# Keeping the transposed w1 of two expert layers in DRAM between two feedforwards, and clearing k's grouped rows in parts

## The chip, the cores and the metric

The kernel runs on one core of one Trainium2 chip. The metric is the device time of one execution in microseconds (us), as the median of several runs. A core has five engines that run their own instruction streams: TensorE (PE in the profile; PEld is its weight load), VectorE (DVE), ScalarE (ACT), GpSimd (POOL) and SyncE (SP), which here only issues DMAs. ScalarE and GpSimd issue DMAs too. All transfers share 16 DMA engines.

## The reference

The input x is 4 x 1024 tokens of 256 values, in float32. The result is

```
x = x + 0.5 * ffn(layernorm(x))
x = x + attn(layernorm(x))
x = x + 0.5 * ffn(layernorm(x))      # the same weights again
```

`ffn` normalizes its input once more to xn and makes q, k and v with three "fast feedforward" layers, then takes softmax(q k^T / 16) v + xn as y, and returns y plus a fourth such layer (f) of y. One fast feedforward is a routed layer: each token walks down a binary tree of depth 8 (255 node vectors), and ends at one of 256 leaves, each with its own little network:

```
for _ in range(DEPTH):
    logit = jnp.einsum('bsd,bsd->bs', x, nw[node]) + nb[node]
    node = 2 * node + 1 + (logit > 0).astype(jnp.int32)
leaf = node - NN
h = act(jnp.einsum('bsd,bsdl->bsl', x, w1[leaf]) + b1[leaf])      # w1: 256 x 256 x 16
return jnp.einsum('bsl,bsld->bsd', h, w2[leaf]) + b2[leaf]        # w2: 256 x 16 x 256
```

The weights of q, k, v and f are the same in both feedforwards. `attn` is a multi-head attention with rotary positions and a page-wise causal mask; the change does not touch it.

## The kernel before, in words

`ffn` (L822) is called twice, with `first=True` (L1687) and `first=False` (L1689), with `attention` between them.

**Routing.** `routes` (L382) goes over the 4096 tokens in eight steps of four tiles of 128 tokens. A step transposes the tokens (L331), multiplies them with all node vectors at once (L340), compares, and finds the leaf by two more matrix products (L354, L366). `routes` overlaps four steps and calls a function `before(k)` once per step, in which other work is woven in.

**Placing and scattering.** `place` (L493) counts the tokens per block of eight leaves and gives each token a row, so that each block's rows fill whole tiles of 128. `scattering` (L580) writes the tokens to these rows of a DRAM buffer `xs` with indirect DMAs from GpSimd (L573), a tile each. `xs` has 63 tiles of rows; rows with no token must be zero, so in the first feedforward `clear` (L268) writes zeros over them first. q and v share one `xs` buffer, k has its own (`xs[1]`).

**w1.** The first weights of the leaves are needed with the 256 inputs on the partitions. `load_first` (L625) makes this out of four parts of 1 MB each (`raw`, two buffers): a part is transposed in four groups of four 128x128 transpositions on TensorE (L636), each group copied out of PSUM by ScalarE (L641) or VectorE (L639) into the SBUF tile `w1` (one buffer, 4 MB). When a part is used up, the next is loaded (L643, L601). The third part waits until the first has been transposed. The 16 groups are woven into a routing, three per step from step 1 on: q's into k's routing (`beside`, L932), k's into v's routing (`building`, L963). v's is made in one go after k's leaves.

**Leaves.** `leaves` (L668) goes over the grouped tiles. For each it loads the rows (`xg`, L677, four tiles ahead), transposes them (L683), multiplies with the block's w1 (L701) and b1 (L704), masks (L709), transposes (L719), applies the activation (L721), multiplies with w2 (L726), and stores the result to DRAM (`og`, L739). Beside the leaves of q run the placing and the scatters of k; beside those of k the placing and scatters of v. `with_steps` (L854) takes one step of the side work per leaf tile.

**What sets the order.** Outside the last attention of `ffn` a scheduler orders each engine's instructions by its own reckoning, within the dependences; `keep_in_program_order` pins single instructions. SyncE issues its DMAs one after another, in the order that this gives: in the first feedforward x, the clear of q's `xs`, two parts of q's w1, the clear of k's `xs`, then the load of q's tile count into a register (L652), a clear of the spare rows of k's results, two more parts, w2 of q (L591), a clear of the spare rows of q's results, two parts of k's w1, and the first xg. [...]

Of the kernel before, what the change touches and what calls it, by code (L numbers as in the profile page):

```python
# [15 lines left out]
F32 = mybir.dt.float32  # L16
# [55 lines left out]
def macaron_kernel(ctx: ExitStack, tc: tile.TileContext, a: dict, out: bass.AP):  # L72
# [183 lines left out]

    xs += [xs[0], dram.tile([NSLOT, XW + 1], F32, name="xs_f")]
    ytok = dram.tile([NTOK, E], F32, name="ytok")


    SPARE = (48, 53, 58, NGRP)
# [6 lines left out]
    def clear(queue, rows):  # L268
        n, width = rows.shape
        return queue.dma_start(  # L270
            rows.rearrange("(g p) c -> p g c", p=P), bc(zero[:, :width], 1, n // P)
        )
# [220 lines left out]
    def place(pool, oh, acc, rows, gblk, sel):  # L493


        ng = tiles_of(pool, counts(pool, acc, NT))
        yield
        end = ends_of(pool, "gend", ng, 0.0)
        first = first_row(pool, end, ng)
        yield  # L500
        for h in range(2):
            yield from ranks(pool, oh, acc, rows, h * NT // 2, (h + 1) * NT // 2, first)
            yield
        found = []
        yield from blocks_ended(pool, acc, NT, found)
        yield
        tile_blocks(pool, found[0], end, gblk, sel)
# [72 lines left out]
    def scattering(f, slot, rows, n):  # L580

        views = dram_disjoint_views(xs[f], NT)
        for t in range(0, NT, n):
            scatter(f, slot, rows, views, *range(t, min(t + n, NT)))
            yield
# [18 lines left out]
    def load_raw(pool, f):  # L604

        return [load_part(pool, f, *p) for p in PART[:2]]
# [18 lines left out]
    def load_first(pool, f, w1, raws, on_both=True):  # L625

        nb_half = P // EPB
        for k, (hf, c) in enumerate(PART):
# [4 lines left out]
            for l0 in range(0, LW, 4):  # L633
# [9 lines left out]
                    raws.append(load_part(pool, f, *PART[k + 1 + len(raws)]))  # L643
                yield

    PRE = 4
    REGS = 16

# [173 lines left out]
    def ffn(first: bool, last: bool):  # L822
# [3 lines left out]
        def drain(*gens):  # L826
            for g in gens:
                for _ in g:
                    pass
# [6 lines left out]
        with ExitStack() as es:  # L836
# [17 lines left out]
            def with_steps(main, *sides):  # L854
# [3 lines left out]
                    next(side, None)  # L858
                drain(side)

            qs = ExitStack()
            with ExitStack() as ws, banks(0, 8):
                wp, lp = stage(ws, "w", 1), stage(ws, "leaves", 2)
# [7 lines left out]
                with ExitStack() as hs, ExitStack() as rs:  # L871
                    raw = stage(rs, "raw", 1, "right")
                    pp = stage(hs, "place", 1)
                    with ExitStack() as rt:
                        hp = stage(rt, "head", 2)
                        scale = [None] * NT
                        if first:
                            mom = hp.tile([P, NT, 2], F32, name="mom", bufs=1)
                        else:
                            mom = moments[1]  # L880

                        def norms(k):
                            ts_ = range(k * GT, k * GT + GT)
                            if first:
                                t = k * GT
                                nc.sync.dma_start(
                                    xres[:, t : t + GT, :],
                                    a["x"][
                                        t // TPB, (t % TPB) * P : (t % TPB + GT) * P, :
                                    ].rearrange("(i p) e -> p i e", p=P),  # L890
                                )
                                for t in ts_:
                                    rows_moments(hp, mom[:, t, :], xres[:, t, :])
                                sc = both_norms(hp, mom[:, k * GT : k * GT + GT, 1], GT)
                            else:

                                lo = k * GT
                                if lo in (0, NT - TPB):
                                    n = TPB if lo else NT - TPB
                                    sc = both_norms(hp, mom[:, lo : lo + n, 1], n, f"_{n}")  # L900
                                    scale[lo : lo + n] = [sc[:, i : i + 1] for i in range(n)]
                                sc = None
                            for i, t in enumerate(ts_):
                                nc.vector.tensor_scalar(
                                    x_of(t),
                                    xres[:, t, :],
                                    mom[:, t, 0:1],
                                    scale[t] if sc is None else sc[:, i : i + 1],
                                    ALU.subtract,
                                    ALU.mult,  # L910
                                )

                        hot = hots_of(pp, 0, 2)
                        routes(hp, 0, *hot, leaf[0], norms)
                        if first:
                            clear(nc.sync, xs[0])
                        w1 = w1_of(0)
                        ahead = load_raw(raw, 0)
                        if first:
                            tc.keep_in_program_order(clear(nc.sync, xs[1]))  # L920
                        build = load_first(raw, 0, w1, ahead)
                        rows = []
                        drain(place(pp, *hot, rows, gblk[0], sel[0]))
                        going = scattering(0, slot[0], rows, 5)
                        hot = hots_of(pp, 1, 2)

                        if first:
                            b1s = [load_b1(raw, f) for f in range(len(FFFS))]
                            for g in b1s[:2]:
                                next(g)  # L930

                        def beside(k):  # L932
                            drain(islice(build, 3 * (k > 0)), islice(going, 1))
                            if first and k and k % 2 == 0:
                                f = k // 2 - 1
                                drain(b1s[f])
                                if f + 2 < len(FFFS):
                                    next(b1s[f + 2])

                        routes(hp, 1, *hot, leaf[1], beside)  # L940
                        drain(build, going)
                        if first:
                            drain(*b1s)
                        w2 = load_second(nc.sync, wp, 0)
                        if first:
                            tc.keep_in_program_order(clear(nc.sync, osrt[0][SPARE[0] * P :]))
                        what = tree(0, AF.Relu, w1, w2)
                        ahead = load_raw(raw, 1)
                        rows = []
                        with_steps(  # L950
                            leaves(*what),
                            place(pp, *hot, rows, gblk[1], sel[1]),
                            scattering(1, slot[1], rows, 1),
                        )
                        spare_leaves(*what)
                        if first:
                            tc.keep_in_program_order(clear(nc.sync, osrt[1][SPARE[0] * P :]))
                        w1 = w1_of(1)
                        build = load_first(raw, 1, w1, ahead)
                        hot = hots_of(pp, 2, 2)  # L960
                        w2 = None

                        def building(k):  # L963
                            nonlocal w2
                            drain(islice(build, 3 * (k > 0)))
                            if k == 4:
                                w2 = load_second(nc.scalar, wp, 1)

                        routes(hp, 2, *hot, leaf[2], building)
                        drain(build)  # L970

                    raw2 = stage(hs, "raw2", 1)
                    what = tree(1, AF.Relu, w1, w2)
                    ahead = load_raw(raw, 2)
                    ahead += [load_part(raw2, 2, *p) for p in PART[2:]]
                    rows = []
                    with_steps(
                        leaves(*what),
                        place(pp, *hot, rows, gblk[2], sel[2]),
                        scattering(2, slot[2], rows, 1),  # L980
                    )
                    spare_leaves(*what)
                    if first:
                        tc.keep_in_program_order(clear(nc.sync, osrt[2][SPARE[0] * P :]))
                    w1 = w1_of(2)
                    w2 = load_second(nc.scalar, wp, 2)
                    drain(load_first(raw, 2, w1, ahead))
                    tc.no_sync_barrier()
# [741 lines left out]
```

## Time and profile before

| what | value |
|---|---|
| median of three runs | 2568.53 us (2558.93 to 2577.99) |
| the profiled execution | 2818.15 us; its span, from first to last instruction, 2816.4 us |
| TensorE (PE) busy | 2399.0 us, 85% |
| VectorE / ScalarE / GpSimd busy | 1472.2 / 1062.7 / 856.4 us |
| moved by DMA | 321.02 MB, mean 114 GB/s |
| clear of `xs` of q and k | 2 DMAs of 8095.5 KB |
| parts of w1 of q, of k | 8 DMAs of 1024.0 KB each (both feedforwards) |

The profile is of one execution, which is longer than the runs without a profile. Busy times are summed per engine; an instruction that issues a DMA counts as not busy, and its duration is that of the issuing. The timeline gives for each instruction its start, its duration, its engine and line, what is written from what, and in brackets how long the engine was idle before it and who released it. An engine that is not the bottleneck loses nothing by being idle, so a share of busy time says little: the stretch in question has to be looked at.

### The profile page before, as it was taken

The page shows a single profiled execution, that of the slowest core. Times are in us where ns is not written, and L with a number is a line of the kernel's source. Part 1 is how long each engine was busy: PE and PEld are TensorE (multiplying, and loading weights), DVE is VectorE, ACT ScalarE, POOL GpSimd, SP SyncE. Part 2 cuts the span into 40 slices and gives each one's busy share as a digit, 9 for nine tenths or more (in the row PEclk, how much of TensorE's full clock was granted, in tenths as well). Part 3 has the DMA queues.
Part 4 walks back from the last instruction along what each step waited for, and adds up shares of the span by engine and source line. Part 5 has one row for each costly group of instructions (what it writes and reads, how often), then busy time and mean ns, then how long its engine had stood idle before and what let it go on. Part 6 is the DMA issues. An engine that isn't in the chain of part 4 may idle for free. (4 is left out here: it accounts for less than half of the span.)

```text
span 2816.4 us, 43155 instructions
## 1 busy us (share of the span) xinstructions
PE 2399.0 (85%) x14456; PEld 1507.2 (54%) x14456; DVE 1472.2 (52%) x4382; ACT 1062.7 (38%) x2495; POOL 856.4 (30%) x978
## 2 busy tenths in 40 slices
PE   7789887877897879999999999889898887879884
PEld 3466776545565744434343443346667755556573
DVE  8454544333455476666676677445354433335453
ACT  2334343222223324555555555434333432222241
POOL 0431334445443531101101000023304455454443
PEclk9899989988899999999999999899999999889997
DMA  9966676333314410000000000016657753332354
GB/s 272 309 198 203 199 228 188 115 102 112 95 63 155 142 63 1 1 1 1 1 1 1 1 1 1 30 45 203 192 187 228 224 163 97 109 118 59 121 171 154
DMA packets 236343, 321.02 MB, mean 114 GB/s; under 512 B 28337, under 2 KB 207426, under 8 KB 232008
## 3 DMA queue, kind: packets, MB, share of 16 engines
q1 hardware_dynamic: 149328, 169.85, 20.1%
q0 software_dynamic: 38640, 100.90, 11.4%
q10 hardware_dynamic: 48136, 47.26, 5.1%
q8 instruction: 130, 2.13, 0.3%
q14 instruction: 109, 0.89, 0.1%
HBM read 193.40 MB, written 129.33 MB: 115 GB/s over the span
## 5 line engine op out<-in xcount | busy, mean ns | idle before, releaser
L1481 DVE TENSOR_REDUCE mxh<-big 128x1 f32<-128x512 f32 (+3 forms) x768 | 392.9, 551 | 190.4 <-PE big L1473 188.4
L1517 ACT ACTIVATE pTh<-big 128x512 f32<-128x512 f32 (+3 forms) x768 | 341.0, 491 | 289.8 <-PE big L1473 265.5
L1509 PE MATMUL big<-qTh,kTh 32*128 32x512 f32 (+3 forms) x1536 | 400.9, 537 | 1.9 <-ACT pTh L1517 1.6
L1473 PE MATMUL big<-kTh,qTh 32*128 32x512 f32 (+3 forms) x1536 | 399.8, 536 | 2.0 <-ACT kTh L1454 1.8
L709 DVE SCALAR_TENSOR_TENSOR hm<-eid,xg,sm 128x128 f32<-128x128 f32 x399 | 138.0, 346 | 301.3 <-PE sm L704 89.0
L340 PE MATMUL sm<-xT,nwT 128*128 128x512 f32 (+2 forms) x528 | 244.1, 606 | 19.5 <-ACT xT L334 19.2
L790 PE MATMUL two<-kT,qT 128*128 128x512 f32 x512 | 244.7, 623 | 7.7 <-issue 5.5
L818 PE MATMUL sm<-vb,pT 128*128 128x256 f32 x1024 | 236.5, 385 | 2.5 <-DVE vb L1002 1.6
L721 ACT ACTIVATE hid<-sm 128x128 f32<-128x128 f32 x399 | 111.6, 280 | 326.4 <-PE sm L719 187.4
L1509 PEld LDWEIGHTS big<-qTh,kTh 32*128 32x128 f32 x1536 | 143.5, 184 | 156.6 <-issue 126.8
L818 PEld LDWEIGHTS sm<-vb,pT 128*128 128x128 f32 x1024 | 193.0, 193 | 29.3 <-DVE vb L1002 1.8
L685 DVE COPY xgT<-sm 128x256 f32<-128x256 f32 x399 | 166.6, 418 | 41.2 <-PE sm L683 20.1
L728 ACT COPY og<-sm 128x256 f32<-128x256 f32 x399 | 148.7, 373 | 99.6 <-PE sm L726 37.1
L334 ACT COPY xT<-sm 128x512 f32<-128x512 f32 (+1 forms) x130 | 70.1, 582 | 279.8 <-PE sm L331 150.1
L683 PE MATMUL sm<-ident,xg 128*128 128x128 f32 x798 | 162.1, 288 | 13.5 <-DMA xg<-xs 7.2
L340 PEld LDWEIGHTS sm<-xT,nwT 128*128 128x128 f32 x528 | 99.9, 199 | 127.7 <-issue 91.8
L348 DVE TENSOR_SCALAR bits<-sm,thr 128x512 bf16<-128x512 f32 (+1 forms) x132 | 96.4, 733 | 136.3 <-PE sm L340 122.6
L1528 PE MATMUL sm<-pTh,vpad 128*32 128x512 f32 (+3 forms) x1536 | 164.9, 500 | 0.0
L790 PEld LDWEIGHTS two<-kT,qT 128*128 128x128 f32 x512 | 98.2, 202 | 112.5 <-issue 108.2
L813 PE MATMUL sm<-ident,pr 128*128 128x128 f32 x512 | 74.2, 289 | 96.9 <-DVE xn L820 52.6
L798 DVE TENSOR_REDUCE mx<-two 128x1 f32<-128x1024 f32 x64 | 78.3, 1223 | 149.4 <-PE two L790 122.3
L1473 PEld LDWEIGHTS big<-kTh,qTh 32*128 32x128 f32 x1536 | 145.5, 184 | 20.1 <-issue 13.9
(325 smaller groups left out, 4382.4 us busy)
## 6 DMA issues: line engine op xcount, KB each, us to landing
xg<-xs SPq DMA_DIRECT2D x298, 128.5 KB
xs<-zero SPq DMA_DIRECT2D x2, 8095.5 KB
xs_f<-zero ACTq DMA_DIRECT2D x14, 1032.0 KB
xg<-xs_f SPq DMA_DIRECT2D x101, 129.0 KB
os_q<-og SPq DMA_DIRECT2D x101, 128.0 KB
os_v<-og SPq DMA_DIRECT2D x101, 128.0 KB
os_k<-og SPq DMA_DIRECT2D x96, 128.0 KB
raw_q<-in_q_w SPq DMA_DIRECT2D x8, 1024.0 KB
```

Source lines behind the costliest of these rows:

```text
L340: nc.tensor.matmul(pl, nwT[:, c, f, r * P : (r + 1) * P], xT[:, c, :], start=(c == 0), stop=(c == KC - 1),)
L683: nc.tensor.transpose(pa[:, c, :], xg[:, x0 + c * P : x0 + (c + 1) * P], ident)
L685: nc.vector.tensor_copy(xT, pa)
L709: nc.vector.scalar_tensor_tensor(hm, eid, xg[:, lf : lf + 1], ph, ALU.is_equal, ALU.mult)
L728: nc.scalar.copy(og, po)
L790: nc.tensor.matmul(ps[:, n0 : n0 + 512], qT[:, c, i * P : (i + 1) * P], kT[:, c, n0 : n0 + 512], start=(c == 0), stop=(c == KC - 1),)
L818: nc.tensor.matmul(po, pT[:, j, :], vb[:, j, :], start=(j == 0), stop=(j == TPB - 1))
L1473: matmul = nc.tensor.matmul(ps[:, :n], qT[r : r + HPAD, hg, i * P : (i + 1) * P], kT[r : r + HPAD, hg, n0 : n0 + n], start=True, stop=True,)
L1481: nc.vector.tensor_reduce(maxima(b, hg)[:, i, c, u : u + 1], ps[:, :n], AX.X, ALU.max)
L1509: matmul = nc.tensor.matmul(ps[:, off:], kT[r : r + HPAD, hg, j * P : (j + 1) * P], qT[r : r + HPAD, hg, qb * QN + off : (qb + 1) * QN], s ...
L1517: nc.scalar.activation(pT[:, u, off:], ps[:, off:], AF.Exp, scale=1.0 / math.sqrt(HD))
L1528: nc.tensor.matmul(acc[r : r + HPAD, off:], vpads[b % 2][:, j, 4 * hg + 2 * pair + u, :], pTs[pair][:, u, off:], start=(j == 0), stop=(j = ...
```

## The change

Two DRAM buffers `w1s` are added, for q and k. In the first feedforward the finished SBUF tile `w1` of q is written there in eight pieces of 0.5 MB while q's leaves run, one piece in five leaf tiles, beside the placing and scattering of k; the same for k. In the second feedforward `load_first` and the loads of the parts are left out for q and k; eight DMAs bring w1 back from `w1s`. For v and f nothing changes.

The clear of k's `xs` was one DMA ahead of k's routing. It is now four, in steps 4 to 7 of k's routing (14, 14, 14 and 21 tiles of rows).

```diff
+    w1s = [dram.tile([P, KC * NBLK * P], F32, name=f"w1s_{nm}") for nm in FFFS[:2]]
+    PIECES = 8
...
+    def pieces(f, w1):
+        flat = w1.rearrange("p c b u -> p (c b u)")
+        n = flat.shape[1] // PIECES
+        for i in range(PIECES):
+            yield flat[:, i * n : (i + 1) * n], w1s[f][:, i * n : (i + 1) * n]
+
+    def keep_first(f, w1):
+        for here, there in pieces(f, w1):
+            nc.sync.dma_start(there, here)
+            for _ in range(5):
+                yield
+
+    def load_kept(f, w1):
+        for here, there in pieces(f, w1):
+            nc.sync.dma_start(here, there)
+        yield
...
-                        ahead = load_raw(raw, 0)
                         if first:
-                            tc.keep_in_program_order(clear(nc.sync, xs[1]))
-                        build = load_first(raw, 0, w1, ahead)
+                            build = load_first(raw, 0, w1, load_raw(raw, 0))
+                        else:
+                            build = load_kept(0, w1)
...
                         def beside(k):
                             drain(islice(build, 3 * (k > 0)), islice(going, 1))
+                            if first and k >= NT // GT // 2:
+                                n = NSLOT * GT // NT // P * 2 * P
+                                lo = (k - NT // GT // 2) * n
+                                hi = NSLOT if k == NT // GT - 1 else lo + n
+                                tc.keep_in_program_order(clear(nc.sync, xs[1][lo:hi]))
...
-                        ahead = load_raw(raw, 1)
+                        ahead = load_raw(raw, 1) if first else []
...
                             leaves(*what),
-                            place(pp, *hot, rows, gblk[1], sel[1]),
-                            scattering(1, slot[1], rows, 1),
+                            abreast(
+                                chain(
+                                    place(pp, *hot, rows, gblk[1], sel[1]),
+                                    scattering(1, slot[1], rows, 1),
+                                ),
+                                keep_first(0, w1) if first else iter(()),
+                            ),
...
-                        build = load_first(raw, 1, w1, ahead)
+                        build = load_first(raw, 1, w1, ahead) if first else load_kept(1, w1)
```

`abreast` takes one step of each of its generators in turn. k's leaves get the same `abreast`, with v's placing and `keep_first(1, w1)`.

More of the change, by code (lines that the diff above doesn't have):

```diff
@@ L859, in with_steps, with abreast @@
                 drain(side)
+            def abreast(*gens):
+                live = list(gens)
+                while live:
+                    live = [g for g in live if next(g, g) is not g]
+                    yield
             qs = ExitStack()
@@ L978, in ffn @@
                         leaves(*what),
-                        place(pp, *hot, rows, gblk[2], sel[2]),
-                        scattering(2, slot[2], rows, 1),
+                        abreast(
+                            chain(
+                                place(pp, *hot, rows, gblk[2], sel[2]),
+                                scattering(2, slot[2], rows, 1),
+                            ),
+                            keep_first(1, w1) if first else iter(()),
+                        ),
                     )
```

## The prediction

> **What bounds the kernel now.** I read the page first, then the stretches of 10 us over the first feedforward, then SyncE's issue timeline, then TensorE's timeline in both feedforwards. The page says that TensorE is busy 85% of the span, but also where that average hides something else: the first two slices (of 70 us) have the DMA engines at 9 tenths.
>
> ```profile
> span 2816.4 us, 43155 instructions
> ...
> DMA  9966676333314410000000000016657753332354
> ```
>
> SyncE's timeline (start, duration, queue, line, what is moved) is where the first 150 us are decided.
>
> ```profile
> 16.93 1.62 SPq L270 DMA_DIRECT2D xs<-zero  x1
> 19.57 29.24 SPq L601 DMA_DIRECT2D raw_q<-in_q_w  x2
> 48.86 0.48 SPq L270 DMA_DIRECT2D xs<-zero  x1
> 79.12 6.92 SPq L270 DMA_DIRECT2D os_k<-zero  x1
> 90.46 14.84 SPq L601 DMA_DIRECT2D raw_q<-in_q_w  x2
> 105.35 0.43 SPq L591 DMA_DIRECT2D w_q<-in_q_w  x1
> 105.83 13.98 SPq L270 DMA_DIRECT2D os_q<-zero  x1
> 119.93 11.66 SPq L601 DMA_DIRECT2D raw_k<-in_k_w  x2
> 141.09 3.17 SPq L677 DMA_DIRECT2D xg<-xs  x7
> ```
>
> The two loads issued behind q's clear (8.29 MB) hold the queue for 29.24 us[...]. k's clear goes in at 48.86; nothing else is issued until 79.12, because SyncE waits at the load of q's tile count, which the placing of q makes only then. So k's clear fills a gap. It also overshoots: the third part of w1 (issued from 90.46, when its buffer is free) lands late, and TensorE waits 11.01 us for it:
>
> ```profile
> 96.34 1.06 PE L636 MATMUL sm<-ident,raw_q 128*128 128x128 f32 x8
> 108.40 1.09 PE L636 MATMUL sm<-ident,raw_q 128*128 128x128 f32 x4 [11.01 <-DMA raw_q<-in_q_w]
> ```
>
> After that TensorE is the bound up to the first leaf transposition (L683) at 153.59, while the DMA engines finish earlier. In the stretches the last two columns are the DMA share and GB/s:
>
> ```profile
> 130.00:140.00 10.00, 7.09 (x36) 3.87 (x35) 3.63 (x13) 3.44 (x6) 4.81 (x5) 1.00 0.91 335
> 140.00:150.00 10.00, 10.00 (x44) 4.70 (x43) 3.30 (x11) 2.25 (x5) 0.00 (x0) 0.83 0.33 93
> 150.00:160.00 10.00, 6.35 (x43) 3.69 (x40) 6.60 (x35) 2.53 (x4) 0.00 (x0) 0.86 0.12 41
> ```
>
> 93 GB/s for 10 us is 0.93 MB, the seven tiles of xg (7 x 128.5 KB). So everything ahead of xg had landed by about 141, 12 us before TensorE wanted xg.
>
> In the second feedforward there are no clears, and the two routings that w1's transposing is woven into are TensorE's:
>
> ```profile
> 2068.27 1.50 PE L636 MATMUL sm<-ident,raw_k 128*128 128x128 f32 x12
> 2069.61 3.60 PE L340 MATMUL sm<-xT,nwT 128*128 128x512 f32 x8
> ...
> 2080.96 3.70 PE L340 MATMUL sm<-xT,nwT 128*128 128x512 f32 x8
> ...
> 2086.56 3.70 PE L340 MATMUL sm<-xT,nwT 128*128 128x512 f32 x8
> ```
>
> A step with 12 transpositions takes 6.75 us (L340 from 2062.86 to 2069.61), a step without 5.60 (2080.96 to 2086.56).
>
> [...] the 8.29 MB have issues of 1.62 and 0.48 us; so I count bytes instead of durations.
>
> **The change, part by part.** The instruction order of the changed kernel shows no other movement than the following.
>
> 1. *Second feedforward, taken away:* 32 groups of 4 transpositions (L636) and their 32 copies, half for q, half for k; 8 loads of 1 MB. On TensorE a full step saves 6.75 - 5.60 = 1.15 us. Per w1: four full steps 4.6, the last step with 4 transpositions about 0.5, the first step about 2 (its transpositions took 2.77, less the 0.7 in which TensorE would wait for xT): 7 us. Two of them: 14 us. The copies are on VectorE and ScalarE, which have gaps there; nothing for them. Bounds: for q, GpSimd's scatters are next: 32 at 1.27 us from 1878 end at 1919, xg is back about 1924, and TensorE (1943.3 less 10.2 of waits labelled "remote" and for xT in 1893 to 1930, less 7) would be ready at 1926; it just fits. So 7 to 14, and up to 22 if the 7.74 us wait at 1900.73 was owed to the part loads. I take 14.
> 2. *Second feedforward, added:* 16 loads of 0.5 MB. q's are issued when attention ends (about 1812) and needed at 1943; the DMA share from 1820 to 1880 is 0.00 to 0.01. k's 4.2 MB come after q's last leaf (2038), 15 us at 285 GB/s, ahead of xg on the queue; needed at 2093, so the routing of v covers them. Cost 0. If they were not covered, 15 us each.
> 3. *First feedforward, w1 written out:* 2 x 4.2 MB on SyncE's queue. Two pieces (1.05 MB) go ahead of the fourth part load, counted in 4. Six fall in q's leaf loop, one in five leaves, ahead of an xg load; 3.15 MB at 285 GB/s are 11 us of DMA time in a stretch (160 to 220) with share 0.72 to 0.97. xg is loaded four leaves ahead (about 5 us) and a piece takes 1.8 us, so most hides. Bounds 0 and 11; I take 3. k's eight go between the part loads while v is routed: DMA share 0.49, 0.47, 0.80, 0.94, 0.06 in 240 to 290, so 15 us fit in the gaps before xg's next loads at 296.78. Cost 0, at most 10.
> 4. *First feedforward, k's clear moved:* all four parts stand behind one another in the order, after the fourth part load and ahead of w2, the clear of os_q, both raw_k and xg. They have no pacing of their own: the part load waits for TensorE, and once it goes (about 98) all four follow. Gain: the third part load now finds an empty queue (90.5 plus about 5), so the 11 us wait goes and TensorE would be ready for the leaves at 153.6 - 11 = 142.6. Loss: by 80 us before had moved 21.9 MB (sum of the stretches); after can have moved only the 15.8 MB issued by then (constants 0.13, node weights 1.05, x 4.19, clear 8.29, raw 2.1), done at 58.6, and the engines stand still till 79. What was left of k's clear at 79 before was 24.05 - 21.65 = 2.4 MB; after it is all 8.29. With 1.05 MB of w1 that is 6.9 MB more ahead of xg. From 79 to 141 before moved 19.4 MB, 313 GB/s; so 22 us more, and some 2 us of gaps while SyncE waits for TensorE around 90: raw_k lands at 141 + 24 = 165 and the first leaf transposition is at 166 instead of 153.6. The wait for a part load has become a longer one for xg. The profiled span loses 12.5. Two waits of before, 2.9 us at 138.89 and part of the 11, may be of the profiled execution alone; without the first, before starts its leaves at 150.7 and the loss is 15.5. I take 14. Bounds: -11 (xg not held) and +18.
>
> What is late next: with the leaves of q starting later, k's placing, its scatters and everything after move by as much; the scatters wait for all clear parts, which are over by then.
>
> Sum: -14 + 0 + 3 + 14 = +3. Against the profiled execution: 2818.15 + 3 = 2821. The runs are shorter than it (2568.53); the view of waits has many labelled "remote" (ScalarE xT 111.1 us, VectorE xn 112.4 us) that I suppose are part of the difference, which no view proves. The places above are not among them but for the two waits named, so I carry the sum over: 2568.5 + 3 = 2572.
>
> **The rivals.**
> *xg is not held up* (w2, the clears and raw_k finish quicker than the bytes say[...]). For: 335 to 373 GB/s at 120 to 140. Against: what must land from 79 on is 25.9 MB (os_k 2.0, parts three and four 2.1, w1 out 1.05, clear 8.3, w2 4.2, os_q 2.0, raw_k 2.1, 32 scatters 4.2), and at 350 GB/s that still ends at 153. Time: -14 - 11 + 3 = -22, 2546; to pass 1% it needs a few us more from the second feedforward.
> *The writes of w1 are exposed* (slower): the DMA engines become the bound of the leaf loop and of v's routing. 8.39 MB at 285 GB/s are 29 us, with 14 from the clear and -14: +29, 2598. It decides when over three quarters of these bytes fail to hide. For: share 0.97 at 160 to 170; against: 0.06 at 280 to 290.
> *q's gain in the second feedforward is eaten by GpSimd's scatters:* -7 + 17 = +10, 2579.
> *The parts of the clear don't do what they say:* spread over the steps, they would collide less; the order shows them together, so this is in the forecast.
>
> **How the numbers follow.** About 1% (25 us) is what a measurement can tell from no change. Forecast (2560 to 2585): 0.60. xg not held: 0.18, of which more than half stays within 1%. Scatters: 0.11, within. Writes exposed: 0.11, nearly all slower. With a tail of larger gains in the second feedforward: faster 0.14, same 0.74, slower 0.12. Range 2546 to 2596, from the first rival to just short of the second.
>
> **What would show it.** Right: no wait for raw_q near 97; DMA share near 0 in 60 to 79, then full to about 165; TensorE's longest early wait before L683 and for xg, ending near 166; routings of k and v in the second feedforward at 5.6 us per step, with 7 us less each. Wrong: L683 before 150 (xg not held); leaves of q or k with gaps of 2 us at each w1s piece; xg late at 1943 less 7.

## The result and the profile after

| | median | range | runs |
|---|---|---|---|
| before | 2570.01 us | 2558.93 to 2577.99 | 4 |
| after | 2602.67 us | 2597.67 to 2606.91 | 4 |

The ratio is 1.0139, with a 95% interval of 1.011 to 1.0167: the changed kernel is slower by 36 us (28 to 43). The forecast was 2572 and its range ended at 2596. The profiled execution of the changed kernel took 2604.91 us, so this time the profile is of an execution like the others.

The changed kernel's page; in the last rows the third digit, 130 to 195 us, is what counts (TensorE at 4 tenths, the DMA engines at 9):

```profile
span 2603.1 us, 42840 instructions
...
PE   6948998899998979999999999988989889999984
...
DMA  8797778544425510000000000041566883442365
```

SyncE's timeline of the changed kernel, in the columns of before's:

```profile
78.82 0.38 SPq L273 DMA_DIRECT2D os_k<-zero  x1
90.40 0.33 SPq L604 DMA_DIRECT2D raw_q<-in_q_w  x1
91.51 0.80 SPq L659 DMA_DIRECT2D w1s_q<-w_q  x2
97.37 0.33 SPq L604 DMA_DIRECT2D raw_q<-in_q_w  x1
97.76 33.17 SPq L273 DMA_DIRECT2D xs<-zero  x4
130.97 9.83 SPq L594 DMA_DIRECT2D w_q<-in_q_w  x1
140.85 13.66 SPq L273 DMA_DIRECT2D os_q<-zero  x1
154.61 5.49 SPq L604 DMA_DIRECT2D raw_k<-in_k_w  x2
```

SyncE waits 5.0 us for TensorE ahead of the fourth part load and issues nothing else from 92.3 to 97.37. The four parts of k's clear go in together behind that load, as forecast, and hold SyncE for 33.17 us; w2, q's spare rows, k's raw parts and xg queue up behind them. TensorE's timeline shows what this leads to:

```profile
96.28 1.51 PE L639 MATMUL sm<-ident,raw_q 128*128 128x128 f32 x12
...
170.39 0.69 PE L706 MATMUL sm<-ident,xg 128*128 128x128 f32 x2 [34.00 <-DMA xg<-xs]
```

All 12 transpositions at 96.28 go without a wait for raw_q. But TensorE stands still for 34.00 us until the first xg has landed, at 170.39. The stretches of the changed kernel (the columns are the stretch, its length, busy time of PE, PEld, DVE, ACT and POOL, TensorE's granted clock, of which 1.00 is full speed, DMA share and GB/s):

```profile
60.00:70.00 10.00, 8.16 (x35) 3.99 (x34) 9.07 (x36) 4.49 (x8) 0.00 (x0) 1.00 0.03 7
70.00:80.00 10.00, 5.47 (x42) 2.40 (x41) 7.48 (x42) 2.53 (x4) 0.00 (x0) 0.94 0.02 7
...
140.00:150.00 10.00, 0.00 (x0) 0.00 (x0) 0.00 (x0) 0.00 (x0) 0.00 (x0) 0.50 1.09 278
150.00:160.00 10.00, 0.00 (x0) 0.00 (x0) 0.00 (x0) 0.00 (x0) 0.00 (x0) 0.50 1.09 386
160.00:170.00 10.00, 0.00 (x0) 0.00 (x0) 0.00 (x0) 0.00 (x0) 0.00 (x0) 0.50 1.02 385
```

The DMA engines do next to nothing for 20 us (7 GB/s) and are then the only ones at work for 30 us (a share of 1.02 to 1.09). The signs that the prediction named for the moved clear are there, though the DMA share is only 0.71 in 80 to 90 us and the wait ends at 170 instead of 166. So the mechanism was seen, and yet the time is 31 us off. The experiments had to find out where those are.

### The profile page after: what moved, and what is told of

It reads as the page before. It is cut to its first block, busy times and chain, and to the rows that moved or that the text cites. A ratio compares the mean times of both kernels' runs of the same rounds, so it can differ in the third digit from the quotient of the medians.

```text
span 2603.1 us, 42840 instructions
## 1 busy us (share of the span) xinstructions
PE 2329.0 (89%) x14286; PEld 1473.6 (57%) x14328; DVE 1457.8 (56%) x4366; ACT 1050.1 (40%) x2479; POOL 861.5 (33%) x978
## 5 line engine op out<-in xcount | busy, mean ns | idle before, releaser
L343 PE MATMUL sm<-xT,nwT 128*128 128x512 f32 (+2 forms) x528 | 240.1, 598 | 8.7 <-ACT xT L337 8.7
L813 PE MATMUL two<-kT,qT 128*128 128x512 f32 x512 | 232.7, 598 | 6.7 <-issue 4.6
L841 PEld LDWEIGHTS sm<-vb,pT 128*128 128x128 f32 x1024 | 190.0, 190 | 26.5 <-DVE pT L837 1.4
L343 PEld LDWEIGHTS sm<-xT,nwT 128*128 128x128 f32 x528 | 97.8, 195 | 117.8 <-issue 89.5
L576 POOL DMA_INDIRECT xs<-xn,slot_v x64 | 61.3, 958 | 202.2 <-DMA os_k<-og 173.8
```

The lines of the kernel that those rows point to most:

```text
L343: nc.tensor.matmul(pl, nwT[:, c, f, r * P : (r + 1) * P], xT[:, c, :], start=(c == 0), stop=(c == KC - 1),)
L813: nc.tensor.matmul(ps[:, n0 : n0 + 512], qT[:, c, i * P : (i + 1) * P], kT[:, c, n0 : n0 + 512], start=(c == 0), stop=(c == KC - 1),)
L841: nc.tensor.matmul(po, pT[:, j, :], vb[:, j, :], start=(j == 0), stop=(j == TPB - 1))
```

## The experiments

Three sessions; in each, the kernel before ran on the same chip (medians 2567.27, 2566.35 and 2566.85 us). "First leaf" is the start of the first leaf matmul of q in the profiled execution (L701 before, L724 after), "q loop" the time from there to the start of the last one with w2 (L726, L749).

| kernel | median us | ratio to before (95%) | first leaf | q loop |
|---|---|---|---|---|
| before, second profile | 2568.17 (one run) | | 141.7 | 68.3 |
| before, third profile | 2557.30 (one run) | | 142.2 | 66.5 |
| the change | 2602.67 | 1.0139 (1.011 to 1.0167) | 172.9 | 75.2 |
| only the clear moved | 2603.24 | 1.0142 (1.0119 to 1.0165) | 174.4 | 67.9 |
| only w1 kept | 2558.15 | 0.9967 (0.9954 to 0.998) | 148.4 | 67.3 |
| a third of the clear late | 2574.01 | 1.0026 (1.0014 to 1.0038) | 156.2 | 70.1 |
| clear late, gap filled | 2581.59 | 1.0062 (1.0042 to 1.0082) | 160.7 | 67.2 |
| clear in q's leaf loop | 2581.91 | 1.007 (1.0047 to 1.0093) | 142.4 | 91.4 |
| only k's w1 kept | 2557.19 | 0.9966 (0.9951 to 0.998) | 140.7 | 68.2 |
| clear late, only k's w1 kept | 2590.76 | 1.0089 (1.0074 to 1.0104) | 172.7 | 68.4 |
| w1 kept, pieces pinned | 2565.10 | 0.9995 (0.9981 to 1.0008) | 140.9 | 74.4 |
| w1 kept, pieces on ScalarE's queue | 2563.90 | 0.999 (0.9972 to 1.0009) | 148.1 | 69.2 |

Spans of one kernel differ by some 10 us between executions (2566.3 and 2555.5 for the kernel before), so times from single traces are compared only stage by stage, and kernels by their ratios.

### Is the profile of before like its runs?

The kernel before was profiled a second time, and later, when the rest was known, a third time.

> The kernel before, unchanged, for a second profiled execution. If the waits labelled remote belong to the first profiled execution alone, this one takes about 2570 us, has few or none of them, and shows where the leaves of q really start (150 to 151 by the forecast's reckoning, against 170.4 in the changed kernel). If they belong to the kernel, it takes about 2818 us again.

> The kernel before, unchanged, profiled a third time. Of its two profiled executions so far one has the wait of 11.0 us for the third part of w1 (and 2816 us of span), the other no such wait (2566 us). Theory: the wait belongs to executions that are disturbed as a whole; with a span near 2566 there is no wait for raw_q over 1 us and the first leaf transposition L683 is at 137 to 139. Rival: the third part load is at the edge in the typical run as well, and a wait of 4 to 11 us shows with a span near 2566.

The second execution took 2568.17 us with a span of 2566.3, the third 2557.30 with 2555.5. No wait labelled "remote" is left. TensorE's timeline of the second:

```profile
98.79 1.51 PE L636 MATMUL sm<-ident,raw_q 128*128 128x128 f32 x12
...
138.01 0.42 PE L683 MATMUL sm<-ident,xg 128*128 128x128 f32 x2
```

and of the third:

```profile
98.38 1.06 PE L636 MATMUL sm<-ident,raw_q 128*128 128x128 f32 x8
100.09 0.69 PE L636 MATMUL sm<-ident,raw_q 128*128 128x128 f32 x4 [0.66 <-DMA raw_q<-in_q_w]
...
138.49 0.41 PE L683 MATMUL sm<-ident,xg 128*128 128x128 f32 x2
```

The 11.01 us for the third part of w1, on which the prediction built, are not there: 0 and 0.66 us. The leaves begin at 138.0 and 138.5, not at 153.59. Two stretches show that the DMA engines had been slower in the first profiled execution:

```profile
80.00:90.00 10.00, 8.97 (x39) 6.95 (x40) 6.19 (x24) 3.63 (x5) 4.97 (x5) 0.73 1.09 234
90.00:100.00 10.00, 7.40 (x40) 4.85 (x39) 3.77 (x9) 1.68 (x3) 7.70 (x8) 1.00 1.07 311
```

The same stretches in the second profile:

```profile
80.00:90.00 10.00, 7.18 (x29) 5.70 (x29) 7.02 (x35) 3.24 (x4) 3.32 (x4) 0.66 1.07 327
90.00:100.00 10.00, 10.00 (x55) 6.78 (x54) 5.13 (x12) 4.35 (x8) 7.56 (x9) 1.00 0.75 251
```

At a share over 1 the engines moved 234 GB/s in the one and 327 in the other. Part of this is what was moved: in the first, more of k's clear was still under way, because by 80 us only 21.9 MB had been moved, against 22.9 (sums of the stretches). In the second the share falls to 0.75, and the third part load, issued at 92.91, goes out at a share of 0.42 (92 to 94 us). So the wait belongs to the one execution that took 2818 us. What disturbed that execution, the profile does not say.

### Which half of the change costs

Only the clear moved, and only w1 kept:

```diff
-                        if first:
-                            tc.keep_in_program_order(clear(nc.sync, xs[1]))
...
+                            if first and k >= NT // GT // 2:
+                                ...
+                                tc.keep_in_program_order(clear(nc.sync, xs[1][lo:hi]))
```

> The kernel before with only the clear of k's rows moved, in four parts; w1 is transposed twice as before. Theory (the moved clear holds up xg): the first leaf transposition at about 166 to 170, 16 to 20 us later than before, and nothing else changes: 2586 to 2592 us, ratio 1.006 to 1.009. Rival (the write-out and read-back of w1 costs the time): within 5 us of before, ratio 1.000 to 1.002, or faster. If the clear alone explains the whole measured loss plus the saving of the second feedforward (33 + 12), 2615, ratio 1.017.

> The changed kernel with the clear of k's rows put back to its old place, as one DMA ahead of k's routing; w1 of q and k is written out and read back as in the change. Theory (the clear costs, w1 saves): the first leaf at about 150, the second feedforward's two routings 11 to 14 us shorter: 2556 to 2560 us, ratio 0.994 to 0.996. Rival (write-out and read-back cost): 2580 us or more, ratio 1.004 or more.

The clear alone takes 2603.24 us, 36 us more than before, more than my theory gave it. TensorE's timeline of this kernel has the same wait:

```profile
172.38 0.69 PE L683 MATMUL sm<-ident,xg 128*128 128x128 f32 x2 [34.77 <-DMA xg<-xs]
```

Against 138.0 that is 34 us later. The kept w1 alone is faster than before by 9 us (5 to 12), as expected. Added together that would be +28; the change has +36. The 8 us between them lie within what the three intervals leave open, but the q loop of the change is 7 us longer than that of the moved clear alone, which the later experiments take up.

### Is it the bytes, the place, or the empty gap?

First, two thirds of the clear at the old place and one third late:

```diff
+                            tc.keep_in_program_order(clear(nc.sync, xs[1][: 42 * P]))
...
+                            if first and k == 4:
+                                tc.keep_in_program_order(clear(nc.sync, xs[1][42 * P :]))
```

> The changed kernel with 42 of the 63 tiles of k's clear in the gap at 49 to 79 us (ahead of k's routing) and 21 after the fourth part load. Theory: the third part load is no longer held up and the bytes ahead of xg are fewer than at the change, so the leaves of q start at 140 to 148: 2546 to 2554 us, ratio 0.991 to 0.994. Rival (write-out and read-back cost): no faster than 2575.

A miss: 2574.01 us, close to the rival's bound, but the trace puts the loss on the clear. Twenty-one late tiles (2.8 MB) are enough for a wait for xg:

```profile
150.40 0.69 PE L706 MATMUL sm<-ident,xg 128*128 128x128 f32 x2 [14.23 <-DMA xg<-xs]
```

There is no free room for them behind the fourth part load: 21 late tiles make 14 us of waiting, 63 make 34 (two pieces of w1 are ahead of xg in both).

Second, the clear late as in the change, but w2 and the clear of q's spare rows, which stand behind it in the change, put into the gap:

```diff
+                            ahead = load_raw(raw, 0)
+                            w2 = load_second(nc.sync, wp, 0)
+                            tc.keep_in_program_order(clear(nc.sync, osrt[0][SPARE[0] * P :]))
```

> The change with k's clear late as it is, but the load of w2 (4.2 MB) and the clear of os_q (2 MB) moved to the place that k's clear had. Theory: what the change loses is the use of the 20 us in which the DMA engines stand still (60 to 79), and 6.2 of 8.3 MB then go there again; only some 2 MB more than in the kernel with the clear at its old place are ahead of xg, 7 us, so the first leaf matmul is at 150 to 156 and the time 2560 to 2570. Rival: it is k's clear itself, at its late place ahead of xg, that costs (in four parts, or among the scatters): then the first leaf stays near 172 and the time at 2595 or more.

Half of the loss is back (2581.59 us, first leaf at 160.7), and not as much as I expected. The wait:

```profile
154.36 0.69 PE L706 MATMUL sm<-ident,xg 128*128 128x128 f32 x2 [17.75 <-DMA xg<-xs]
```

The reason for the rest is in the stretches. In this kernel, w2 and the spare rows (6.2 MB) go out in the gap:

```profile
60.00:70.00 10.00, 8.16 (x36) 4.03 (x35) 9.13 (x37) 4.49 (x8) 0.00 (x0) 1.00 1.09 385
70.00:80.00 10.00, 6.51 (x42) 2.54 (x41) 6.74 (x38) 2.53 (x4) 0.00 (x0) 0.82 0.35 124
```

In the kernel before (second profile) it is the clear that goes out there:

```profile
60.00:70.00 10.00, 8.13 (x35) 3.97 (x33) 7.02 (x29) 3.00 (x6) 0.00 (x0) 0.83 1.11 285
70.00:80.00 10.00, 7.76 (x48) 3.28 (x45) 7.74 (x37) 4.01 (x7) 0.00 (x0) 1.00 1.09 297
```

Both have the engines full in 60 to 70, but 385 GB/s against 285. The clear's 8.29 MB at 285 are 29 us of DMA time; 6.2 MB at 385 are 16 us, so they fill less of the gap. The next two stretches of the gap-filled kernel are not full either:

```profile
80.00:90.00 10.00, 8.50 (x32) 6.20 (x32) 6.07 (x25) 3.22 (x4) 4.65 (x5) 0.67 0.74 249
90.00:100.00 10.00, 10.00 (x57) 6.93 (x55) 5.62 (x16) 5.91 (x9) 7.55 (x9) 1.00 0.83 277
```

From 60 to 100 us the shares add up to 4.02 in the kernel before (second profile), 3.33 with a third of the clear late, 3.01 here and 1.69 in the change. So 7, 10 and 23 us of DMA time less were used than before, and the first leaf transposition comes 12, 16 and 32 us later than at 138.0. Unused DMA time is the larger part of the delay in all three kernels. The rest, 5 to 9 us, holds the two pieces of w1 ahead of xg (1.05 MB; some 3 us is my estimate, from the 293 to 386 GB/s in 90 to 100 and 150 to 170 us of the change) and the late clear's lower rate (244 to 278 GB/s in 110 to 150 us of the change); these were not separated further. The loss went by DMA time left unused, and bytes measured it only at the rate at which they moved (285 and 385 GB/s above). Whether the clear's rows of 257 floats are the reason for its lower rate was not tried.

Third, the clear behind the first xg loads, nine parts of 7 tiles between the leaves of q:

```diff
+                                    place(pp, *hot, rows, gblk[1], sel[1]),
+                                    clearing(xs[1], 7) if first else iter(()),
+                                    scattering(1, slot[1], rows, 1),
```

> The change, but k's clear neither in the gap nor in the routing: nine parts of 7 tiles, one per leaf, in q's leaf loop between the end of k's placing and k's scatters, so behind the first xg loads on SyncE's queue and ahead of later ones. Theory: what hurts is what stands ahead of xg on the one queue. The loop then starts on time (first L724 at 141 to 143), but the 8.3 MB take some 31 us at the 265 GB/s at which they went in the changed kernel, in a stretch whose DMA share was already 0.7 to 0.9; xg falls behind in the loop by about 20 us instead, and the time is 2565 to 2580. Rival A: a clear behind the first loads is hidden, 2552 to 2558. Rival B: it costs as much as ahead of xg, 2595 or more, because k's scatters have to wait for it and GpSimd is then the bound.

The leaves start at 142.4, as in the kernel before, and the loop takes 91.4 us instead of 66.5 to 68.3. What waits in it, from the waits of that kernel between 141 and 235 us:

```profile
PE sm L706 <- DMA xg<-xs: 9.1, 8, 3.0
PE sm L724 <- issue: 5.7, 2, 3.2
```

The wait has only been cut into pieces, and the granted clock in 180 to 200 is 0.50. The time, 2581.91, is just over the top of what I gave it. So the same bytes do not hold up the start of the leaves when they stand behind the first xg loads on SyncE's queue (142.4, against 172.9 in the change). But order and moment changed together here: the clear is issued from 158 us on. A late clear on another engine's queue, which would separate the two, was not run. Of the places tried for the clear, only the gap hides it.

### What the kept w1 brings, and what it costs

Only k's w1 kept, q's transposed again, the clear at its old place:

```diff
-                                keep_first(0, w1) if first else iter(()),
+                                iter(()),
```

> k's clear at its old place, and only k's w1 kept; q's is transposed again in the second feedforward. The traces so far put q's gain there at 3 us and k's at 8.5. Theory: before less 8.5 is 2558.7, and nothing early is disturbed, so 2557 to 2560, the same as with both kept (2558.2), since q's gain of 3 is paid for by the early wait. If q's pieces cost less than q's gain in the typical run, this is slower than 2558.2 by up to 3 us.

It takes 2557.19 us, as much as with both kept. The net gain is k's, as far as these medians tell (each interval is some 4 us to either side). In the second feedforward, from the start of q's last leaf matmul to that of k's first, the traces without k's w1 kept have 60.6, 58.5 and 58.4 us, those with it 52.0 to 52.2. Q's stage, from the first token transposition beside q's 16 groups to the first xg, takes 54.25, 54.30 and 54.25 us where w1 is transposed and 51.07 and 51.20 where it is kept: 3.1 us. Its first step shows why so little. Before (second profile):

```profile
1746.39 1.97 PE L331 MATMUL sm<-ident,xn 128*128 128x128 f32 x8
1748.15 2.59 PE L636 MATMUL sm<-ident,raw_q 128*128 128x128 f32 x12
1750.58 3.60 PE L340 MATMUL sm<-xT,nwT 128*128 128x512 f32 x8
1754.02 1.04 PE L331 MATMUL sm<-ident,xn 128*128 128x128 f32 x8
```

With w1 kept and the clear at its old place:

```profile
1748.33 1.97 PE L334 MATMUL sm<-ident,xn 128*128 128x128 f32 x8
1750.97 6.08 PE L343 MATMUL sm<-xT,nwT 128*128 128x512 f32 x8 [0.67 <-ACT xT L337]
1756.89 1.04 PE L334 MATMUL sm<-ident,xn 128*128 128x128 f32 x8
```

Transpositions in the slow first microseconds took 2.59 us; without them, L343 runs there and takes 6.08 instead of 3.60. The step is longer by 0.93 us (8.56 against 7.63; 8.6 to 9.1 in the seven traces with q's w1 kept, 7.6 to 8.2 in the six without). At the start the first transpositions take 1.97 instead of 1.04 us. How long the clock stays low is read from stretches of 1 us in the same stage of the first profile of before and of the change. In the one the granted clock is 0.50 in 1876 to 1880 us, 0.55 in the next and 1.00 from 1881 on, 5 us after the first token transposition (1876.07). In the other it is 0.50 up to 1802, 0.71 in the next and 1.00 from 1803 on, 8 us after it (1794.84); L343 takes 6.21 there. So the work taken out of the slow start saved nothing there: the slow start lasted longer. TensorE stood idle for 0.67 us in it (0.68 in the change), waiting for xT; whether that prolonged it was not tried.

The same on top of the late clear:

> The change with k's clear late as it is, but only k's w1 kept. The moved clear alone took 2603.2 us, and the changed kernel, with both w1 kept, 2602.7: the kept w1 is worth nothing there, while it is worth 9 with the clear at its old place. Theory: in the changed kernel q's pieces fall one by one into q's leaf loop and cost it some 7 us (75 us against 68), more than q's gain of 3; without them k's gain stays: 2593 to 2597. Rival: what is missing is lost elsewhere (k's pieces, the second feedforward): 2600 or more.

It takes 2590.76 us, 13 us less than the change by the ratios (1.0089 against 1.0139), a little below my 2593. Without q's pieces the q loop is back at 68.4 us from 75.2. So in the change q's kept w1 costs more than it brings. The traces account for some 4 of the 13 us (7 in the loop, less the 3.1 of the second feedforward); the rest is open, and the two intervals allow 5 to 21. In the change the pieces fall between the leaves, from 175 on; with the clear at its old place the scheduler sets six of them together behind the first seven xg loads, and the loop takes 67.3. Two variants of that kernel, with the writes alone edited: each piece held in its place in the leaf loop, and all pieces on ScalarE's queue.

```diff
-            nc.sync.dma_start(there, here)
+            tc.keep_in_program_order(nc.sync.dma_start(there, here))
```

> The kept w1 with k's clear at its old place (2558.2 us), but each written-out piece held to its place in the leaf loop, so that none goes ahead of the fourth part load. Theory: the two early pieces are what makes TensorE wait for the third part load in that kernel (4.2 us, and 1.9 us of slow clock after it); with them gone the first leaf matmul L724 is at about 142 instead of 148.4, and the time is 2552. Rival: pieces that fall one by one into the leaf loop cost that loop some 7 us, as they seem to in the changed kernel (75 us from the first L724 to the last L749, against 67 to 68 where there are none or where they stand together): then the wait goes but the loop takes 75, and the time stays at 2558.

```diff
-            nc.sync.dma_start(there, here)
+            nc.scalar.dma_start(there, here)
```

> The kept w1 with k's clear at its old place, all pieces of q and k written out on ScalarE's queue instead of SyncE's. Theory that it is the place on SyncE's queue that hurts: no wait for the third part load, leaf loop of q 67 to 68 us, time 2552. Rival, that it is the bytes that hurt: the third part load is still some 4 us late, because the pieces go out as soon as their half of w1 is there; time 2558 or more, and more than that if ScalarE's copies are held up by the issues.

Pinned, the first leaf is at 140.9 instead of 148.4: the wait for the third part is gone. But the loop takes 74.4 us, as in the change, and the time is 2565.10, no better than before. The rival was right on the loop. At the end of k's loop this trace is level with that of only w1 kept (345.9 and 345.5 us); the 7 us by which its ratio is worse come later, and what costs them was not found. The waits of this kernel from 140 to 216 us:

```profile
PE sm L706 <- DMA xg<-xs: 4.9, 5, 2.1
PE sm L724 <- issue: 3.7, 3, 1.3
```

On ScalarE's queue the wait for the third part stays, though no piece stands on SyncE's queue:

```profile
102.08 1.09 PE L639 MATMUL sm<-ident,raw_q 128*128 128x128 f32 x4 [5.17 <-DMA raw_q<-in_q_w]
```

In the kernel with pieces on SyncE's queue it was 4.24 us, and there the pieces were issued behind the third part, not ahead of it:

```profile
91.33 0.34 SPq L604 DMA_DIRECT2D raw_q<-in_q_w  x1
92.45 0.89 SPq L659 DMA_DIRECT2D w1s_q<-w_q  x2
```

So it is their bytes beside the part load that hurt, at a time when the engines are full (shares of 0.92 to 1.15 in the stretches of 92 to 106 us with the pieces on SyncE's queue, 1.03 in 90 to 110 with them on ScalarE's); a place behind the load on its queue did not keep them from delaying it. Together the pieces of q cost some 6 to 8 us wherever they go, ahead of the leaves or between them.

Two of the kernels with the clear in its old place are thus faster than the kernel before: w1 kept for both (0.9967) or only for k (0.9966); the second does it with half the traffic. With the pieces pinned or on ScalarE's queue (0.9995, 0.999) no gain can be told.

## Why the prediction was wrong, point by point

**Step 4, the clear, failed by its size.** The mechanism is as predicted (no wait for raw_q, an idle gap, then xg late), but "I take 14" should have been 32: 170.39 less 138.01. The step took "the first leaf transposition is at 166 instead of 153.6" from a profiled execution whose early stage was itself late. Of the 153.59, 11.01 us were the wait for the third part, 2.91 the wait at 138.89, and 1.7 after each of them the slow clock (granted 0.50 in 109 to 112 us and 0.60 in the next, where L340 took 5.34 instead of 3.60; 0.50 to 0.74 in 140 to 144, where it took 5.40 instead of 3.70): 17.4 together. TensorE had come to the third part 2.4 us earlier than in the second profile (96.34 against 98.79), so 15 are left, of the 15.6 that are 153.59 less 138.01. The prediction noticed that the 2.91 and "part of the 11" "may be of the profiled execution alone", and took 14 where its sum without the first gave 15.5. The 11.01 it kept whole, and credited their removal as a gain. They were never lost in the typical run, so nothing was there to be gained. The other 4.4 us are 170.39 against 166: the bytes ahead of xg were priced at the mean of 313 GB/s, while the changed kernel moved 26.5 MB from 80 to 170 us (sum of the stretches), 295 GB/s, which is some 5 us more.

The warning was on the page: 2818 us profiled against 2568 as the median. "The places above are not among them but for the two waits named, so I carry the sum over": that was the wrong inference. The 11.01 us carried the label of a wait for raw_q, and the two other executions had 0 and 0.66 us in that place.

**Step 1 was half right.** 14 us were forecast, 7 per w1. K's stage gave 6.3 to 8.6. Q's gave 3.1: the first step counted as "about 2" lost 0.93 instead, the second gave 0.36 instead of 1.15, and only the later ones gave what was counted. GpSimd's scatters did not take q's gain; it was never there.

**Step 2 was right.** No wait of TensorE for w1 as read back shows in the second feedforward; k's stage has its full gain.

**Step 3 was too low.** "I take 3": the q loop grew by 7 (75.2 against 68.3). K's loop, counted at 0, took 69.1 us in the change and 66.2 to 67.7 where no w1 is written out, 1 to 3 more; this part is not clear of noise, since the kernel with a third of the clear late writes k's w1 too and takes 66.1.

The sum with the measured terms is -10 + 0 + 9 + 32 = +31, against 36 (28 to 43). The nearest rival in time, the writes of w1 exposed (2598), came near by a wrong way: it counts 29 us for the writes, which cost 9. The rival "xg not held" is refuted by the 34.00 us.

## What to carry to other kernels

When the profiled execution is far from the median of the runs, no wait of it may be credited as a gain until a second profile shows it as well. A transfer that fills an idle stretch between full ones can be free there: with k's clear, about 29 us of DMA time, in the gap, TensorE waited 0 and 0.66 us for the next part load (second and third profile), and the clear made the leaves start 34 us later or their loop last 23 to 25 us longer where it was moved. Ask what else would fill the gap before it is moved. Work saved in the first microseconds after a pause of TensorE can be worth nothing, when what follows runs at the slow clock in its place: without 2.59 us of transpositions, L343 took 6.08 us instead of 3.60.

## What the runs showed of the hardware

At a DMA share over 1, the engines moved 285 to 297 GB/s of the clear of rows of 257 floats (second profile of the kernel before, 60 to 80 us), and 385 GB/s of w2 and the spare rows in rows of 256 floats (gap filled, 60 to 70 us). Single issues on SyncE took 0.33 to 0.38 us in the change (78.82, 90.40 and 97.37 us). For the same 8.29 MB of k's clear the one issue of before took 0.48 us, and the four of the change, behind the fourth part load, 33.17 us; the issue of the next load took 9.83. With pieces issued 1.1 us behind a part load on the same queue, TensorE waited 4.24 us for that load. After a pause the granted clock was full again 5 us after the first token transposition in the kernel before (first profile, 1876 to 1881 us) and 8 us after it in the change (1795 to 1803 us).
